# Attention and a routed mixture of experts: the first expert's first 512 rows in two slots, one of them gathered during the attention

## The chip, the cores and the metric

The kernel runs on one core of a Trainium2 chip. The metric is the device time of one execution in microseconds (us). Of the kernel before there are three runs and one profiled execution.

The engines are called by the names of the profile: PE is TensorE, whose weight loads have a row of their own (PEld), ACT is ScalarE, DVE is VectorE, POOL is GpSimd and SP is SyncE. SP computes nothing here: it issues transfers. POOL computes a little and issues the indirect transfers, gathers and scatters, whose rows are named by an index each.

## The reference

The input `x` has B = 4 elements (batches) of T = 1024 rows of C = 256 numbers. What is computed, cut to what matters:

```python
# 1. attention, 16 heads of 16, causal, keys and queries from down- and up-projections, half of each head rotated
x = layernorm(x + attention(x))
# 2. a mixture of 8 experts, two for each row
scores = (x @ router_w.T + router_b) / temperature     # (b, t, 8)
for _ in range(3):                                      # Sinkhorn, over experts and then over rows
    log_alpha = log_alpha - logsumexp(log_alpha, axis=-1)
    log_alpha = log_alpha - logsumexp(log_alpha, axis=-2)
gates = exp(log_alpha) / (sum + 1e-08)
topk_gates, topk_idx = top_k(gates, 2)                  # renormalised
out_e = (relu(x @ wg[e]) * (x @ wp[e])) @ wo[e]         # 256 -> 512 -> 256
x = layernorm(x + sum over the two picks of gate * out_e)
```

The Sinkhorn normalisation runs over the 1024 rows of an element, so the experts of an element's rows are known only when the attention of the whole element is done. It also spreads the rows evenly: an expert gets about 256 pairs (row, expert) of each element.

## The kernel before, in words

**Order.** All engines' instructions are put in order by a scheduler when the kernel is built, from the order in which the program issues them, their priorities and estimated durations. The program is written as generators ("lanes") that yield a cost after each step; the attention loop hands out budgets to them. A step's place on its engine is fixed from then on: an engine runs in order, and where one instruction waits, all behind it wait.

**Attention.** The main loop (L1152 to L1217) goes over units of four heads, four units per element; in the last element, b = 3, the later half of the queries is done first, then the first half in two units. In each, scores and exponentials (`s`, `sT`, `pT`) and the products with the values (`y`, L440) alternate, and masks are put on by POOL (`pT`, L478). Beside the attention of element b run the end of element b - 1 (`finish`, L585: projection, layer norm, its rows stored to `x1_rows` and `results`, router logits) and its routing (`route`, L711). SP loads queries and keys (`qs`, `ks`, L339).

**Routing.** `route` does three rounds of Sinkhorn steps, each with turns of PE (`sk_tp`, L774), ACT and DVE, then the top two, then positions: each pair (row, expert) gets a place in its expert's region of a list `pairs` in memory. `so_ps` (L840 to L845, PE) counts the pairs ahead of each, `base` (L852, DVE) is the number of places used by the elements so far, `so_i` (L863) the index. `scatter` (L866) writes the pairs of an element there with 16 indirect transfers on POOL (L873), as `S0` to `S3` in the lane `places`. After element 2, `base` is raised to 512 for each expert (`floor`, L853), so that the first 512 places of each region hold pairs of elements 0 to 2 alone, and can be worked on while element 3 is still routed.

**Slots.** The experts' work is cut into slots: eight `first` ones of 512 rows (the first 512 places of the eight regions), eight `second` ones (places 512 to 1023), and 256-row slots for what lies beyond, of which three always run. A slot

- takes its list: one load on SP for all eight first slots (`ents`, L974), one for the second eight, and one for each 256-row slot (`ent`, L967);
- gathers its rows with one indirect transfer per 128 rows (`xg`, L985, POOL; two buffers);
- loads its weights (L1011, SP, three transfers of 512 KB) and splits them into high and low halves (`wh` on ACT L191, `wl` on DVE L192), six of each per expert;
- transposes its rows on PE (`xgT_ps`, L1030) and splits them (`xh`, `xl`);
- for each of four quarters of the 512 hidden numbers multiplies into `gp` and `lp` (three fp32 matmuls for each product, L198 to L200), then relu and product (L1047 ACT, L1048 DVE), and the halves `hh` and `hl`;
- multiplies by `wo` into `eo`, scales by the gate (L1065, ACT), and adds the result to `results` with an indirect transfer (L1066, POOL). These adds wait for those of the slot before.

The rows, lists and halves of a slot are prepared between the quarters of the slot before it (`begin`, L1235). In slots of 512 rows `gp` and `lp` have a PSUM bank each, in slots of 256 rows they share one.

**The first slot and the end of the attention.** `begin_early` (L1145) issues the list's load, the weights' loads and the gather of the first slot. The main loop calls it (L1208) when the routing of element 2 is done and all its scatters are out, and if that doesn't come to pass, it is called after the loop. The transposes of the first slot follow (`rows(first[0], ...)`), then the pools of the attention are closed, the split weights go where its buffers were, and the slots begin. What is left of element 3, `finish`, `route` and the table of slots (`lay_out`), is issued here.

**The second eight slots.** The scatters of element 3 (`S3`) are handed out in the slots 0_5 and 0_6 by the table `PLACES`, and what is left at the end of slot 0_6. The load of the second list waits for the last of them, and the gathers of the second slots wait for this list. The order of the second slots is 1_7, 1_6, ... 1_0; the first has the weights of 0_7.

After the last slot the results are read back, added and normalised (L1268 and following).

Of the kernel before, what the change touches and what calls it, by code (L numbers as in the profile page):

```python
# [12 lines left out]
I32 = mybir.dt.int32  # L13
# [20 lines left out]
P = 128  # L34
# [7 lines left out]
def kernel(  # L42
# [16 lines left out]
    nc = tc.nc  # L59
    B, T, C = x_in.shape  # L60
# [3 lines left out]
    E, _, FF = wg_in.shape  # L64
# [11 lines left out]
    scale = 1.0 / math.sqrt(DH)  # L76

    BT = B * T


    ER = 512
    SR = 256
    REGION = BT + SR
    NOVER = (2 * BT - 4 * ER + 2 * (SR - 1)) // SR
    NLIST = (E - 1) * REGION + 2 * ER + NOVER * SR
    NLIST += -NLIST % P

    const = ctx.enter_context(tc.tile_pool(name="const", bufs=1))
# [59 lines left out]
    for half in range(NQC):  # L148
# [13 lines left out]
        out=mask, in_=mask, pattern=[[-1, P]], compare_op=ALU.is_ge, fill=MASKED, base=0, channel_multiplier=1,  # L162
# [5 lines left out]
        out=reach, in_=reach, pattern=[[1, P]], compare_op=ALU.is_ge, fill=MASKED, base=0, channel_multiplier=-1,  # L168
# [34 lines left out]
    for n in range(3):  # L203
        acc = any_tile(f"weffT{n}")
        for i in range(H // 2):
            at = i % 4 * 2 * DH
# [287 lines left out]
    pairs = dram.tile([NLIST, 4], I32, name="pairs")  # L494
    results = dram.tile([BT + ER, C], F32, name="results")
    x1_rows = dram.tile([BT, C], F32, name="x1_rows")

    rank = const.tile([P, E], F32, name="rank")
    base = const.tile([P, E], F32, name="base")
    floor = const.tile([P, E], F32, name="floor")  # L500
    for e in range(E):
# [10 lines left out]
        out=before, in_=before, pattern=[[1, P]], compare_op=ALU.is_gt,  # L512
# [7 lines left out]
    def prepare():  # L520
# [10 lines left out]
        nc.vector.tensor_single_scalar(no_pair[:, :, 0], no_pair[:, :, 3], ER - 1, ALU.bitwise_and)  # L531
        nc.vector.tensor_single_scalar(no_pair[:, :, 1], no_pair[:, :, 0], BT, ALU.bitwise_or)
        nc.vector.memset(no_pair[:, :, 2:4], 0)
        nc.gpsimd.dma_start(out=pairs.rearrange("(p n) w -> p n w", p=P), in_=no_pair)
        nc.gpsimd.dma_start(
            out=results[BT:].rearrange("(n p) c -> p n c", p=P),
            in_=none.unsqueeze(1).to_broadcast([P, ER // P, C]),
# [38 lines left out]
    def apart(what, kind, ins, others):  # L576

        seen = no_deps.setdefault(what, {})
        for o in others:
            for i in seen.get(o, ()):  # L580
                tc.declare_no_dep(ins.ins, i, reason="they touch rows of their own")
        seen.setdefault(kind, []).append(ins.ins)
# [127 lines left out]
    def route(b):  # L710
# [9 lines left out]
        for it in range(SINKHORN_ITERS):  # L720
            m = tiny("sk_m")
# [7 lines left out]
            s = tiny("sk_s")  # L729
# [33 lines left out]
                out=ws, in0=tp[:E, P : 2 * P], in1=wt, scale=1.0, scalar=0.0, op0=ALU.mult, op1=ALU.add,  # L763
# [16 lines left out]
        s = tiny("tk_s")  # L780
# [12 lines left out]
        for k in range(2):  # L793
            m = tiny(f"tk_m{k}")
# [55 lines left out]
        )  # L850
        yield 0.0
        nc.vector.tensor_tensor(base, base, ps[:, NE : NE + E], ALU.add)  # L852
        if b == B - 2:  # L853
            nc.vector.tensor_tensor(base, base, floor, ALU.max)
        at = sinkp.tile([P, 2, NB], F32, tag="so_a", name=f"so_a{b}")
# [11 lines left out]
    def scatter(b, ent, ati):  # L867

        for n in range(NB):
            for k in range(2):  # L870
                while not hole[0]:
                    yield WAIT
                ins = nc.gpsimd.indirect_dma_start(  # L873
                    out=pairs[:, :],
                    out_offset=bass.IndirectOffsetOnAxis(ap=ati[:, k, n : n + 1], axis=0),
                    in_=ent[:, n, k, :], in_offset=None,
                )
                in_turn(ins)
                after(ins, latest[0])
                apart("pairs", "last" if b == B - 1 else "write", ins, ("last", "write", "early"))  # L880
                yield 1.0 if b == B - 1 else SCAT3 if ending[0] else SCAT


    def tab(name, shape):
# [66 lines left out]
    class Slot:  # L951


        def __init__(self, which, s):
            self.which, self.s, self.name = which, s, f"{which}_{s}"
            self.rows = SR if which == 2 else ER
            self.blocks = self.rows // P
            self.raw, self.hl = [None] * 3, [None] * 3
            self.like = None

    lists = {}

    def pairs_of(k):
        if k.which == 2:
            row = value(1, k.s, NLIST - SR)
            k.ent = const.tile([P, k.blocks, 4], I32, name=f"ent_{k.name}")
            nc.sync.dma_start(  # L967
                out=k.ent, in_=pairs[bass.ds(row, SR)].rearrange("(p j) w -> p j w", j=k.blocks)
            )
            return  # L970
        if k.which not in lists:
            ent = lists[k.which] = const.tile([P, E, k.blocks, 4], I32, name=f"ents{k.which}")
            regions = pairs[: E * REGION].rearrange("(e r) w -> e r w", r=REGION)
            ins = nc.sync.dma_start(  # L974
                out=ent.rearrange("p e j w -> p e (j w)"),
                in_=regions[:, k.which * ER : (k.which + 1) * ER].rearrange("e (p j) w -> p e (j w)", p=P),
            )
            if not k.which:
                apart("pairs", "early", ins, ("last",))
        k.ent = lists[k.which][:, k.s]  # L980
# [102 lines left out]
    def drain(gen):  # L1083
        for _ in gen:
            pass
# [41 lines left out]
    early = project(1, 0, bg_tile)  # L1127
# [6 lines left out]
    lane, side, places = Lane(), Lane(), Lane()  # L1134
# [2 lines left out]
    lane.add("prepare", prepare())  # L1137
    budget = {0: (8.0, 8.0, 8.0, 11.3), 1: (9.5, 9.5, 6.0, 11.3), 2: (9.5, 9.5, 6.0, 0.0)}
    budget[B - 1] = (12.0, 4.0, 0.0, 0.0, 8.0, 8.0)
    first = [Slot(0, e) for e in range(E)]  # L1140
    second = [Slot(1, e) for e in reversed(range(E))]
    second[0].like = first[-1]
    further = [Slot(2, n) for n in range(NOVER)]
    early = None
# [7 lines left out]
    routed = [0]  # L1152
    ahead = sum(len(gs) * sum(HG * BPQ * (qc + 1) for qc in qcs) for _, gs, qcs in units)
    for i, unit in enumerate(units):
        b, gs, qcs = unit
        g = gs[0]
        last = b == B - 1
        nth = i - [u[0] for u in units].index(b)
        ends = last and qcs == (0,)
        if nth == 0 and b > 0:  # L1160
            if b == 1:
                lane.until("P2h0")
            elif b == 2:
                lane.until("P3h0")
            lane.add(f"F{b - 1}", finish(b - 1))
            if b + 1 < B:
                lane.add(f"P{b + 1}", project(b + 1, 1, bg_tile))
            if last:
                lane.until(f"P{b}")
                pctx.close()  # L1170
                late_pool[0] = pctx.enter_context(tc.tile_pool(name="late", bufs=1, reuse_waits="tile"))
        if nth == (2 if last else 1) and b > 0:
            lane.until(f"F{b - 1}")
        if ends and g == 0:
            lane.add("F", finish(b, range(1, NQC)))
        if g == 3 and b + 2 < B:
            lane.add(f"P{b + 2}h0", project(b + 2, 0, bg_tile))
        steps = len(gs) * sum(HG * BPQ * (qc + 1) for qc in qcs)
        give = budget[b][nth]
        for n, over in enumerate(attend(unit)):  # L1180
            attended_to += not over
            if i + 2 < len(units):
                if units[i + 2][0] != units[i + 1][0]:
                    if n == 30:
                        lane.until(f"P{b + 1}")
                        load_stack(units[i + 2])
                elif n == 4:
                    load_stack(units[i + 2])

            lead = min(LEAD, HG * BPQ + 2 * attended_to, SLIM + 0.65 * max(0, ahead - 64 - attended_to))  # L1190
            while maxed < attended_to + lead:
                with tc.high_priority(offset=PR[0]):
                    step = next(maxima, None)
                if step is None:
                    break
                maxed += step
            with tc.high_priority(offset=PR[1]):
                lane.give(give / steps)
            if routed[0] < b and not any(m == f"F{b - 1}" for m, _ in lane.todo):
                routed[0] = b  # L1200
                side.add("R", route(b - 1))
            at = n - HG * BPQ * (len(qcs) - 1)
            hole[0] = ends or qcs[-1] > 0 and HOLE[0] <= at < HOLE[1]
            ending[0] = ends
            with tc.high_priority(offset=PR[2] if last else 0):
                side.give(SIDE3 if last else SIDE)
                places.give(1.0)
            if last and routed[0] == b and not side.todo and not places.todo and early is None:  # L1208
                early = pctx.enter_context(early_pool())
                begin_early()  # L1210
        if nth == NG - 1:
            attended[b] = True
# [4 lines left out]
    if early is None:  # L1217
        early = pctx.enter_context(early_pool())
# [35 lines left out]
    def run(keys, given=()):  # L1254
        drain(begin(keys, 0, given))
        for n, key in enumerate(keys):
            slot(key, begin(keys, n + 1, given))
            if key is first[E - 2]:
                places.until(f"S{B - 1}")

    run(first + second + further[:SURE], (0,))
# [134 lines left out]
```

## Time and profile before

| | us |
|---|---|
| median of three runs | 1074.82 |
| the three runs | 1073.68, 1074.82, 1082.69 |
| the profiled execution, its own time | 1075.18 |
| its span in the profile | 1073.4 |
| PE busy in the span | 976.7 (91%) |
| DVE busy | 734.0 (68%) |
| ACT busy | 626.3 (58%) |
| POOL busy | 476.0 (44%) |
| last y matmul of the attention, first gp matmul | 696.31, 697.96 |
| first and last scatter of element 3 (start) | 808.56, 842.44 |
| first transpose of the second list's rows | 852.07 |

The profiled execution took 1.8 us more than its span, which runs from the first to the last instruction that was recorded. Times in the views are microseconds from the start of the span. In a timeline a row has the start, the duration of the group, the engine, line, operation, output and inputs with their shapes, and how many instructions were taken together; in brackets stands how long the engine was idle before it, and what it waited for. "PEclk" is the clock that was granted to PE, in tenths of full speed or as a share. A matmul's start-to-start distance tells what it costs; its own duration is longer, since matmuls are pipelined.

### The profile page before, as it was taken

How to read it: one execution, taken by the hardware profiler on the slowest of the kernel's cores; microseconds unless marked ns; L12 is line 12 of the kernel's file. 1: busy time of each engine (PE TensorE's matmuls, PEld its weight loads, DVE VectorE, ACT ScalarE, POOL GpSimd, SP SyncE). 2: the span in 40 equal slices, each digit the busy share in tenths (PEclk: the TensorE clock that was granted, in tenths of full speed). 3: DMA queues.
4: the chain of work that ended last, by engine and by line, in shares of the span. 5: the costliest groups of instructions: out<-in, count | busy, mean ns of one | idle time of the engine just before them, and what ended most of it. 6: DMA issues, size and time to landing. Idle time of an engine off the chain costs nothing.

```text
span 1073.4 us, 18121 instructions
## 1 busy us (share of the span) xinstructions
PE 976.7 (91%) x6440; PEld 608.2 (57%) x6440; DVE 734.0 (68%) x1627; ACT 626.3 (58%) x1314; POOL 476.0 (44%) x543
## 2 busy tenths in 40 slices
PE   5688999999999999999999998999999699999960
PEld 3554443455544445543344344488888588888860
DVE  4777877888888888798657884085767245555636
ACT  3445666765666656676656675565656245555633
POOL 6174261121352622453233215526557675664535
PEclk9899999999989999999999999899999799999995
DMA  6563331220330412323332220356653464755637
GB/s 252 167 214 96 111 107 35 80 95 26 129 93 33 124 48 73 114 55 109 81 104 84 52 80 2 87 181 159 149 140 92 97 143 110 185 115 125 142 58 313
DMA packets 71363, 119.67 MB, mean 111 GB/s; under 512 B 16416, under 2 KB 43040, under 8 KB 70880
## 3 DMA queue, kind: packets, MB, share of 16 engines
q1 hardware_dynamic: 48544, 81.76, 24.0%
q0 software_dynamic: 20672, 36.41, 15.5%
q8 instruction: 53, 0.87, 0.3%
q10 hardware_dynamic: 2048, 0.27, 0.2%
q14 instruction: 46, 0.38, 0.1%
HBM read 82.52 MB, written 35.60 MB: 110 GB/s over the span
## 4 chain that ended last, share of the span: by engine, by line
PE 76%; DVE 6%; DMA 6%; ACT 5%; issue 3%; SPq 3%; POOL 1%; ACTq 0%; POOLq 0%; DVEq 0%
PE y L440 14%; PE s L354 11%; PE sT L460 11%; PE gp L200 3%; PE gp L199 3%; PE eo L198 3%; PE gp L198 3%; PE eo L199 3%; PE eo L200 3%; PE po L640 3%; SPq L339 2%; ACT pT L471 2%; PE lp L200 2%; PE lp L199 2%; PE lp L198 2%
## 5 line engine op out<-in xcount | busy, mean ns | idle before, releaser
L471 ACT ACTIVATE pT<-sT 128x512 f32<-128x512 f32 (+1 forms) x608 | 327.8, 576 | 175.5 <-PE sT L460 125.4
L375 DVE TENSOR_REDUCE mx<-s 128x1 f32<-128x384 f32 (+3 forms) x352 | 216.3, 633 | 34.9 <-PE s L371 33.5
L460 PE MATMUL sT<-qs,ks 98*128 98x512 bf16 (+3 forms) x768 | 216.4, 331 | 11.3 <-ACT pT L471 8.5
L354 PE MATMUL s<-ks,qs 96*128 96x512 bf16 (+3 forms) x768 | 212.2, 331 | 15.5 <-DMA ks<-parts 8.3
L384 DVE TENSOR_REDUCE mx<-s 128x1 f32<-128x512 f32 x256 | 171.2, 682 | 43.6 <-PE s L354 41.0
L478 POOL TENSOR_SCALAR_AFFINE_SELECT pT<-pT 128x512 f32<-128x512 f32 x112 | 70.8, 638 | 253.3 <-ACT pT L471 245.7
L440 PE MATMUL y<-pT,va 128*32 128x512 f32 (+3 forms) x1536 | 172.8, 505 | 2.4 <-POOL pT L478 1.5
L1066 POOL DMA_INDIRECT results<-eo,ents x64 | 104.6, 1635 | 80.2 <-ACT eo L1065 60.6
L354 PEld LDWEIGHTS <-qs 96*128 96x128 bf16 x768 | 71.0, 99 | 120.6 <-issue 90.6
L460 PEld LDWEIGHTS <-ks 98*128 98x128 bf16 x768 | 70.2, 100 | 90.1 <-issue 58.0
L873 POOL DMA_INDIRECT pairs<-ent,so_i x64 | 67.9, 1061 | 67.5 <-ACT pT L471 49.2
L1048 DVE TENSOR_TENSOR relu<-relu,lp 128x512 f32<-128x512 f32 x64 | 43.8, 685 | 63.2 <-PE lp L200 33.1
L371 PE MATMUL s<-mask,ident_b 128*128 128x128 bf16 (+2 forms) x352 | 86.6, 247 | 0.0
L192 DVE TENSOR_TENSOR wl<-w,wh 128x512 fp32r<-128x512 f32 x108 | 69.7, 684 | 19.6 <-ACT wh L191 17.1
L198 PE MATMUL eo<-wh,hh 128*128 128x256 f32 x280 | 81.2, 291 | 0.9 <-ACT eo L1065 0.6
L199 PE MATMUL eo<-wl,hh 128*128 128x256 f32 x280 | 79.4, 285 | 0.0
L985 POOL DMA_INDIRECT xg<-x_rows,ents x64 | 64.5, 1008 | 33.5 <-issue 17.0
L1047 ACT ACTIVATE relu<-gp 128x512 f32<-128x512 f32 (+1 forms) x76 | 42.8, 563 | 62.4 <-PE gp L200 38.4
L200 PE MATMUL eo<-wh,hl 128*128 128x256 f32 x280 | 77.8, 284 | 0.0
L440 PEld LDWEIGHTS y<-pT,va 128*32 128x32 f32 x1536 | 32.2, 108 | 63.5 <-issue 44.5
L191 ACT CAST wh<-w 128x512 fp32r<-128x512 f32 x108 | 60.4, 618 | 11.0 <-PE gp L199 7.3
L192 DVE TENSOR_TENSOR hl<-relu,hh 128x512 fp32r<-128x512 f32 (+1 forms) x76 | 48.6, 647 | 26.3 <-ACT hh L191 21.3
(222 smaller groups left out, 1870.9 us busy)
## 6 DMA issues: line engine op xcount, KB each, us to landing
ks<-parts SPq DMA_DIRECT2D x90, 128.0 KB
w<-in_wg_dram SPq DMA_DIRECT2D x18, 512.0 KB
w<-in_wp_dram SPq DMA_DIRECT2D x18, 512.0 KB
w<-in_wo_dram SPq DMA_DIRECT2D x18, 512.0 KB
qs<-parts SPq DMA_DIRECT2D x66, 128.0 KB
parts<-lv POOLq DMA_DIRECT2D x12, 384.0 KB
parts<-lv POOLq DMA_DIRECT2D x24, 192.0 KB
xh<-in_x_t_dram SPq DMA_DIRECT2D x8, 512.0 KB
```

Source lines behind the costliest of these rows:

```text
L192: (sub or nc.vector).tensor_tensor(lo, src, hi.bitcast(F32), ALU.subtract)
L198: nc.tensor.matmul(ps, lhsT=sh, rhs=mh, start=(i == 0), stop=False)
L199: nc.tensor.matmul(ps, lhsT=sh, rhs=ml, start=False, stop=False)
L200: nc.tensor.matmul(ps, lhsT=sl, rhs=mh, start=False, stop=(i == n - 1))
L354: nc.tensor.matmul(ps, lhsT=q(h, half)[:NROW, t * P : (t + 1) * P], rhs=k(h, kc)[:NROW, :w], start=first, stop=last,)
L371: nc.tensor.matmul(each[:, :, w - P :], lhsT=ident_b, rhs=mask.unsqueeze(1).to_broadcast([P, m, P]), start=False, stop=True,)
L375: nc.vector.tensor_reduce(mx_of[:, half, h0 : h0 + m, t], each, AX.X, ALU.max)
L384: nc.vector.tensor_reduce(mx_of[:, kc, h, t : t + 1], ps, AX.X, ALU.max)
L440: nc.tensor.matmul(acc[g, qc][SLOT * h : SLOT * (h + 1), lo:], lhsT=va[b % 2][:, kb, at : at + SLOT], rhs=pT[:, h, lo:], start=(kb == 0), ...
L460: nc.tensor.matmul(st[:, h % m * w : (h % m + 1) * w], lhsT=k(h, kb // BPQ)[: NROW + 2, kb % BPQ * P : (kb % BPQ + 1) * P], rhs=q(h, qc)[: ...
L471: latest[0] = nc.scalar.activation(pT[:, h + 1 - m : h + 1, lo:], st[:, : m * w].rearrange("p (h t) -> p h t", t=w), AF.Exp, scale=scale,)
L1066: ins = nc.gpsimd.indirect_dma_start(out=results[:, :], out_offset=bass.IndirectOffsetOnAxis(ap=k.ent[:, j, 1:2], axis=0), in_=eo, in_offs ...
```

## The change

The first expert's first 512 places are worked on in two slots of 256 rows, 0_0 and 0_256. After element 1, `base` of expert 0 is raised to at least SR = 256, so that the first 256 places of its region hold pairs of elements 0 and 1 alone. The load of this slot's list is issued at the end of the scatters of element 1, and `begin_early` is called as soon as the loop, in its last element and past the first of its units, finds these scatters gone. Slot 0_256 has a list load and a gather of its own and uses the split weights of slot 0_0. The list `ents` of all first slots is loaded as before, now for 0_1 and the following. Scatters of element 2 and 3 and the list loads have kinds that say which of them touch different places, so that they don't wait for each other. There are nine first slots instead of eight, and the rest of the scatters of element 3 is issued after the last but one of them, which is 0_6 as before.

```diff
@@ route
         nc.vector.tensor_tensor(base, base, ps[:, NE : NE + E], ALU.add)
+        if b == B - 3:
+            nc.vector.tensor_scalar_max(base[:, :1], base[:, :1], float(SR))
         if b == B - 2:
             nc.vector.tensor_tensor(base, base, floor, ALU.max)
@@ scatter
-                apart("pairs", "last" if b == B - 1 else "write", ins, ("last", "write", "early"))
+                kind = "last" if b == B - 1 else "last but one" if b == B - 2 else "write"
+                apart(
+                    "pairs", kind, ins,
+                    ("last", "last but one", "write", "first") + (("early",) if b == B - 1 else ()),
+                )
                 yield 1.0 if b == B - 1 else SCAT3 if ending[0] else SCAT
+        if b == B - 3:
+            pairs_of(first[0])
@@ Slot
-        def __init__(self, which, s):
-            self.which, self.s, self.name = which, s, f"{which}_{s}"
-            self.rows = SR if which == 2 else ER
+        def __init__(self, which, s, at=None):
+            self.which, self.s, self.name, self.at = which, s, f"{which}_{s}" if at is None else f"{which}_{s}_{at}", at
+            self.rows, self.ent = ER if which < 2 and at is None else SR, None
@@ pairs_of
+        if k.ent is not None:
+            return
...
+        if k.at is not None:
+            row = k.s * REGION + k.at
+            k.ent = const.tile([P, k.blocks, 4], I32, name=f"ent_{k.name}")
+            ins = nc.sync.dma_start(
+                out=k.ent, in_=pairs[row : row + k.rows].rearrange("(p j) w -> p j w", j=k.blocks)
+            )
+            if not k.which:
+                apart("pairs", "early" if k.at else "first", ins, ("last",) if k.at else ("last", "last but one"))
+            return
@@ the slots
-    first = [Slot(0, e) for e in range(E)]
+    first = [Slot(0, 0, 0), Slot(0, 0, SR)] + [Slot(0, e) for e in range(1, E)]
+    first[1].like = first[0]
     second = [Slot(1, e) for e in reversed(range(E))]
@@ the main loop
-            if last and routed[0] == b and not side.todo and not places.todo and early is None:
+            if last and nth and not any(m == f"S{B - 3}" for m, _ in places.todo) and early is None:
                 early = pctx.enter_context(early_pool())
                 begin_early()
@@ run
-            if key is first[E - 2]:
+            if key is first[-2]:
                 places.until(f"S{B - 1}")
```

## The prediction

> **What bounds the kernel now.** I read first the slices of the page, to see where TensorE (PE) is not the bound; then, for each of the two holes that the change can reach, the engine's timeline and the chain of waits.
>
> ```profile
> PE   5688999999999999999999998999999699999960
> PEclk9899999999989999999999999899999799999995
> ```
>
> A slice is 26.8 us, the first is slice 0. PE is at 90% or more from slice 4 to 37, but for slice 24 (644 to 671, in the last stretch of the attention) and slice 31 (832 to 859), which is a 6 at clock 7. That hole is the place where the first eight slots give way to the second eight. The chain of waits there:
>
> ```profile
> 829.84 0.37 SPq L1011
> 830.21 14.85 issue
> 845.05 3.26 DMA ents<-pairs
> 848.44 0.73 issue
> 849.17 1.00 POOL xg L985
> ...
> 853.00 2.65 DMA xg<-x_rows,ents
> 855.78 0.47 PE xgT_ps L1030
> ```
>
> SP stands 14.85 us at the load of the second list until the last scatter of the last element has landed; then come the list (3.26 us) and the gathers. POOL's timeline shows what those scatters (L873) wait for:
>
> ```profile
> 806.67 1.58 POOL L1066 DMA_INDIRECT results<-eo,ents  x1 [4.22 <-ACT eo L1065]
> 808.56 1.47 POOL L873 DMA_INDIRECT pairs<-ent,so_i  x1 [0.30 <-DVE upto L905]
> 810.33 2.60 POOL L873 DMA_INDIRECT pairs<-ent,so_i  x1 [0.30 <-issue]
> 813.23 2.37 POOL L873 DMA_INDIRECT pairs<-ent,so_i  x1 [0.30 <-issue]
> 815.91 0.96 POOL L873 DMA_INDIRECT pairs<-ent,so_i  x1 [0.30 <-issue]
> ...
> 842.44 0.98 POOL L873 DMA_INDIRECT pairs<-ent,so_i  x1 [0.30 <-issue]
> ```
>
> POOL goes without a break from 806.67 to 843.42: 16 scatters and five result scatters between them. So the hole's end is set by when POOL begins them and how fast it goes. PE pays:
>
> ```profile
> 852.07 0.45 PE L1030 MATMUL xgT_ps<-ident,xg 128*128 128x128 f32 x1 [7.10 <-DMA xg<-x_rows,ents]
> ...
> 855.78 0.47 PE L1030 MATMUL xgT_ps<-ident,xg 128*128 128x128 f32 x1 [0.76 <-DMA xg<-x_rows,ents]
> ...
> 856.27 0.41 PE L199 MATMUL eo<-wl,hh 128*128 128x256 f32 x1
> ```
>
> Its last matmul before started at 844.57, so nearly 11 us go until the fourth transpose, and then the matmuls of eo are 0.21 us apart instead of 0.12 until about 860.5 (granted clock 0.50 in 850 to 860): 2.0 us more. The other hole is the end of attention, where transposes of the gathered rows stand among the last y matmuls:
>
> ```profile
> 695.27 0.63 PE L440 MATMUL y<-pT,va 128*32 128x256 f32 x6 [0.82 <-ACT pT L471]
> ...
> 696.66 0.55 PE L1030 MATMUL xgT_ps<-ident,xg 128*128 128x128 f32 x3
> ...
> 697.96 0.49 PE L198 MATMUL gp<-xh,wh 128*128 128x512 f32 x1
> ```
>
> **The change part by part.** I set the compiled orders of both kernels side by side, engine by engine.
>
> Early gather. The list of slot 0_0 (SP) and its two gathers (POOL) now stand behind the scatters of element 1, whose last is issued at 611.60. The last scatter of element 3 lands 2.6 us after its issue (842.44 to 845.05), so SP gets past the new load at about 614.2. Behind it on SP stand the six ks loads that wait for PE until 614.61 anyway: cover 0.4 us; without it, attention waits a few us for ks at most. On POOL the gathers come at about 617.5 to 620, ahead of a mask (affine select) that starts at 618.78 after 4.12 us of idle time; it may come 1 us late, and the next one is due only at 622.09. Taken: 0; bounds 0 to 1.5 us, as PE is busy 10 of 10 there.
>
> End of attention. The eight transposes of xg_0 and three of xg_1 leave PE's order between y and the first gp: four pairs of 0.38 to 0.44 and one group of 0.55 us, 2.2 us in all. Four of them go to 678 to 682, where PE has half the clock and ScalarE (ACT) sets the pace. First gp then at 695.9 instead of 697.96: a gain of 2.1. Lower bound 0: ACT's wh casts start at 697.28, right behind its last yT, and could keep the end where it is; upper bound 3.5: the 0.82 of waiting and some of ACT's 3.88 us wait on the transposes (before 694.62) go too.
>
> Slots 0_0 and 0_256 in place of one. 96 matmuls at 256 columns for 48 at 512: 96 x 0.118 less 48 x 0.233 (starts of eo and of gp in the timeline) = +0.1 us. ACT: four more relu and hh at 376 and 396 ns for four at 597 and 620, two more xh: +1.0 us; VectorE (DVE) the same way (418 for 685): +0.7 to 1.2. DVE is 5.00 of 5 us busy in 700 to 705 and 4.98 in 710 to 715, PE 4.94 and 5.00: both bind. Taken 0.5; bounds 0 to 1.2. The new maximum on base is one DVE instruction of 128x1 behind a row of 0.16 us; nothing waits there: 0.
>
> Route of element 3. On PE its positions (so_ps) move ahead of gp_5_0, from behind lp_5_2. By the sum of PE's rows from the first gp, 88.5 instead of 100.2 us; before, that took 6.3 us more than the sum (697.96 + 100.2 = 798.2, but 804.47), so after: 695.9 + 88.5 + 5.6 + 0.5 = 790.5, 14 earlier.
>
> Scatters of element 3. They can't use all of that: POOL has xg_7's gathers and eo_4_0 ahead of them (800.83 before), so 800.83 - 2.1 + 1.57 + 0.3 = 800.6 for the first, 8.0 earlier. Up to the last one's start the order has 15 scatters and four result scatters (4_1, 4_2, 4_3, 5_0; five before). Pitch: the first five take 1.98 each (808.56 to 818.44), the others 1.40; a result scatter 1.9. Sum 5 x 1.98 + 10 x 1.40 + 4 x 1.9 = 31.5: the last is issued at 832.1 (842.44), its data there at 834.7, first gather at 838.8 (849.17), first transpose possible at 841.7, the fourth at 845.4 (855.78).
>
> PE at the second list. It arrives after 137.6 us of rows (139.6 before; 12 matmuls of gp_7_3 and lp_7_3 are moved behind the transposes): 695.9 + 137.6 + 7.4 + 0.5 = 841.4, where 7.4 is the 844.97 - 697.96 - 139.6 of before. So it meets the first block on time and waits three times 0.75 us, to 845.4. From there to the next point that is the same in both orders (transposes of slot 1_6, 872.78 before) are 17.7 us of rows (15.0 before, plus the 2.0 of half clock = 17.0 seen). So 863.1 at full clock, 9.7 earlier; 865.1 with the same loss of clock, 7.7 earlier. Before, stretches with a pause and matmuls between (695 to 698) kept clock 1.00, but 11 us of almost nothing did not; I take the middle, 8.7.
>
> The Trainium skill, "TensorE: Matmul & The Clock Gate", Part 1: The HAM clock gate, says that a window of about 3.4 us without work halves the clock and a busy one restores it; 0.50 in 850 to 860 and 0.97 in 860 to 870 agree. By it a wait of 4 us with four transposes in it need not halve the clock, and the gain would be 9.7, not 8.7.
>
> From 872.78 to the end PE is the bound and the orders are the same, so the gain stays: 1075.18 - 8.7 = 1066.5 against the profiled execution, which is 0.36 above the median of the three runs: **1066.1 us**.
>
> **The rivals.** (a) Scatters at full rate. At the end of attention the same kind of scatters go at 1.26 us (648 to 654). Then the last is issued at 800.6 + 15 x 1.26 + 4 x 1.9 = 827.1, gathers from 833.8, first transpose possible 836.7, before PE arrives at 841.4: no wait, 1_6 at 841.4 + 17.7 + 0.5 = 859.6, gain 13.2: 1061.6. For it: the rows of 0.96 us after 815.91. Against: scatters between result scatters took 1.40.
>
> (b) Scatters slow throughout. The two of 2.60 and 2.37 us fall in 808 to 816, with DVE 7.93 of 8 us busy; element 3's scatters now begin 8 us earlier, next to other DVE work. All at 1.98: last issued 800.6 + 15 x 1.98 + 7.6 = 837.9, fourth transpose 851.2, 1_6 at 870.9 with the loss of clock, gain 1.9: 1072.9. The Trainium skill, "SBUF — State Buffer", SBUF: two separate sides, says that GpSimd can't write its descriptors while DVE holds the port that they share; the two long rows agree, the 0.96 us ones beside an idle DVE too. The same end has the case that the scatters begin no earlier than before, since POOL or ACT holds them: 1073 to 1075.6.
>
> (c) Slower. PE runs in order. Before, so_m was there at 800.28 and PE took it at 804.47, 4.2 us of reserve; now PE comes to it 14 us earlier, while the logits that start the chain come 2.1 + 6.7 = 8.8 earlier and DVE has 3.5 us less of rows ahead of it: reserve about 2.5. If the Sinkhorn steps (each with a turn of PE, DVE and ACT) run later than that, PE stands in slot 4, with all matmuls behind. Up to some 3 us hide in the wait at the second list; from 13 us of lag on the kernel is slower than before, from 24 us by 1%. For 15 us: 1077.
>
> **How the numbers follow.** About 1% (10.75 us) is what a measurement of this kernel tells from no change. Chances: forecast (gain 4 to 10.7) 0.50; (a) 0.26; (b), with the scatters that begin no earlier, 0.16; (c) 0.08, half of it past 1%. Faster by over 1% (below 1064.1) is (a) and a little of the forecast's upper end: 0.30; slower by over 1%: 0.05; within: 0.65. Range: from (a) with the 1.1 us more at the end of attention, 1060.5, to the upper end of (b), 1075.0.
>
> **What would show it.** Right: two gathers at L985 between 615 and 621; no x_rows transposes in 687 to 696 and the first gp at 695 to 697; so_ps near 790 with no idle time of PE before it; the first scatter of element 3 at 800 to 801, the last near 832; PE's wait before the second list's transposes under 5 us instead of 11, and clock above 0.8 there. Wrong: idle time of PE "<-DVE so_m" or "<-DMA ks"; scatters of 2 us throughout; a first gp at 698; DVE as what ends PE's idle time in 700 to 720.

## The result, and the profile after

| | before | changed |
|---|---|---|
| median of the runs beside each other, us | 1076.79 (4 runs) | 1065.97 (4 runs) |
| lowest and highest run, us | 1073.68, 1082.69 | 1061.88, 1070.52 |
| the profiled execution and its span, us | 1075.18, 1073.4 | 1070.52, 1068.7 |
| first gp matmul | 697.96 | 696.04 |
| first and last scatter of element 3 (start) | 808.56, 842.44 | 801.59, 829.67 |
| transposes of slot 1_6 begin | 872.62 | 867.26 |

The ratio is 0.9899, 95% interval 0.9871 to 0.9928: about 1% faster. The profiled execution of the changed kernel is the longest of its four runs and gained only 4.7 us, so this profile shows less gain than the median. The lines of the changed kernel stand lower in the file, by 1 in the attention and in the matmuls of the slots (L199 to L201), by 3 at the scatters of pairs (L876), by 20 in the slots (gathers L1005, transposes L1050, result scatters L1086); in e2 it is two less there, in e5 and e9 to e12 one less.

The slices of the page, changed kernel: the 6 at slice 31 (now 828 to 855) is an 8 with the clock at 9, and slice 25 (668 to 695) has become an 8 beside slice 24.

```profile
PE   6688999999999999999999998899999899999960
PEclk9889999999999999999999999999999999999985
```

The end of the attention on PE's timeline, changed kernel:

```profile
691.91 0.55 PE L615 MATMUL yt_ps<-ident,yT 128*128 128x128 f32 x3
694.38 0.43 PE L441 MATMUL y<-pT,va 128*32 128x128 f32 x8 [1.93 <-ACT pT L472]
694.74 0.44 PE L1050 MATMUL xgT_ps<-ident,xg 128*128 128x128 f32 x2
...
696.04 0.38 PE L199 MATMUL gp<-xh,wh 128*128 128x256 f32 x1
```

The four transposes of slot 0_0 are gone from here (two each at 681.18 and 682.64); the two that are left at 694.74 are of slot 0_256, so the sign of none in 687 to 696 isn't met to the letter. PE stands 1.93 us for ACT before the last y products.

POOL's timeline, changed kernel: the early gather, then the first and the last scatter of element 3 and the first gather of the second list.

```profile
618.63 1.04 POOL L1005 DMA_INDIRECT xg<-x_rows,ent  x1 [1.80 <-DMA ent<-pairs]
619.98 0.96 POOL L1005 DMA_INDIRECT xg<-x_rows,ent  x1 [0.31 <-issue]
620.95 0.64 POOL L479 TENSOR_SCALAR_AFFINE_SELECT pT<-pT 128x512 f32<-128x512 f32 x1
```

```profile
801.59 1.27 POOL L876 DMA_INDIRECT pairs<-ent,so_i  x1 [0.30 <-issue]
...
829.67 0.95 POOL L876 DMA_INDIRECT pairs<-ent,so_i  x1 [0.30 <-issue]
...
836.66 1.01 POOL L1005 DMA_INDIRECT xg<-x_rows,ents  x1 [1.48 <-PE xgT_ps L1050]
```

PE's timeline, changed kernel: the second half of the transposes of slot 0_7, which still has its rows from the first list, and then the first transposes of the second list's rows.

```profile
834.03 0.80 PE L199 MATMUL gp<-xh,wh 128*128 128x512 f32 x1 [2.67 <-ACT xh L192]
...
835.48 1.06 PE L1050 MATMUL xgT_ps<-ident,xg 128*128 128x128 f32 x4
...
848.68 0.60 PE L1050 MATMUL xgT_ps<-ident,xg 128*128 128x128 f32 x4
```

The group at 835.48 is what the first gather of the second list (836.66) waited for. The second list's own four transposes, at 848.68, run as one group without a wait for their rows. But PE had stood 2.67 us for ACT at 834.03, 0.77 and 1.22 us at 811.63 and 814.19, and 0.52 at 829.28: it came to the list late. Whether that belongs to the change was the first question.

### The profile page after: what moved, and what is told of

Same layout as the page of the kernel before. It is cut to its first block, busy times and chain, and to the rows that moved or that the text cites. A ratio compares the mean times of both kernels' runs of the same rounds, so it can differ in the third digit from the quotient of the medians.

```text
span 1068.7 us, 18250 instructions
## 1 busy us (share of the span) xinstructions
PE 973.5 (91%) x6488; PEld 609.0 (57%) x6488; DVE 736.0 (69%) x1638; ACT 626.9 (59%) x1324; POOL 477.4 (45%) x543
## 4 chain that ended last, share of the span: by engine, by line
PE 77%; DVE 6%; DMA 6%; ACT 4%; SPq 3%; issue 2%; POOL 1%; another core or an unknown queue 0%; ACTq 0%; POOLq 0%; DVEq 0%
PE y L441 13%; PE s L355 11%; PE sT L461 10%; PE gp L201 4%; PE gp L200 3%; PE gp L199 3%; PE eo L201 3%; PE eo L199 3%; PE eo L200 3%; PE po L641 3%; SPq L340 3%; PE lp L201 2%; PE lp L200 2%; PE lp L199 2%; ACT pT L472 2%; PE s L372 2%
## 5 line engine op out<-in xcount | busy, mean ns | idle before, releaser
L441 PE MATMUL y<-pT,va 128*32 128x512 f32 (+3 forms) x1536 | 169.9, 500 | 3.6 <-ACT pT L472 1.9
L355 PEld LDWEIGHTS <-qs 96*128 96x128 bf16 x768 | 71.2, 99 | 123.1 <-issue 93.8
L1086 POOL DMA_INDIRECT results<-eo,ents x60 | 100.4, 1673 | 73.4 <-ACT eo L1085 60.3
L876 POOL DMA_INDIRECT pairs<-ent,so_i x64 | 64.3, 1004 | 68.4 <-ACT pT L472 50.1
L1068 DVE TENSOR_TENSOR relu<-relu,lp 128x512 f32<-128x512 f32 x60 | 41.0, 684 | 66.4 <-PE lp L201 25.2
L199 PE MATMUL eo<-wh,hh 128*128 128x256 f32 x280 | 80.7, 290 | 1.3 <-ACT eo L1085 1.3
L201 PE MATMUL eo<-wh,hl 128*128 128x256 f32 x280 | 77.9, 284 | 0.0
L1005 POOL DMA_INDIRECT xg<-x_rows,ents x60 | 61.9, 1031 | 30.3 <-issue 15.2
L199 PE MATMUL gp<-xh,wh 128*128 128x512 f32 (+1 forms) x200 | 70.9, 360 | 2.8 <-ACT xh L192 2.7
L200 PE MATMUL gp<-xl,wh 128*128 128x512 f32 (+1 forms) x200 | 71.6, 359 | 0.0
L201 PE MATMUL gp<-xh,wl 128*128 128x512 f32 (+1 forms) x200 | 70.6, 355 | 0.3 <-DVE wl L193 0.3
```

Of the source, the lines that this page charges most:

```text
L199: nc.tensor.matmul(ps, lhsT=sh, rhs=mh, start=(i == 0), stop=False)
L200: nc.tensor.matmul(ps, lhsT=sh, rhs=ml, start=False, stop=False)
L201: nc.tensor.matmul(ps, lhsT=sl, rhs=mh, start=False, stop=(i == n - 1))
L355: nc.tensor.matmul(ps, lhsT=q(h, half)[:NROW, t * P : (t + 1) * P], rhs=k(h, kc)[:NROW, :w], start=first, stop=last,)
L441: nc.tensor.matmul(acc[g, qc][SLOT * h : SLOT * (h + 1), lo:], lhsT=va[b % 2][:, kb, at : at + SLOT], rhs=pT[:, h, lo:], start=(kb == 0), ...
L1086: ins = nc.gpsimd.indirect_dma_start(out=results[:, :], out_offset=bass.IndirectOffsetOnAxis(ap=k.ent[:, j, 1:2], axis=0), in_=eo, in_offs ...
```

## The experiments

Each has five rounds, with the kernel before on the same chip. The ratios are to that; e1 to e4 ran together on one chip, e5 to e7, e8 to e10 and e11 to e12 on three others.

**e1: the changed kernel once more.**

> The changed kernel as it is, for a second profile. Theory A (what the profile after shows is built into the order of its instructions): about 10 us faster than before (1062 to 1070); PE again stands about 5 us in the stretch in which slot 0_6 passes to 0_7 (808 to 836 in the first profile), among it 2 to 3 us for ACT's xh, and doesn't wait for the second list. Theory B (those waits were an accident of that run): PE's waits there under 1.5 us, and the time nearer to 1062.

1059.01 us against 1072.70, ratio 0.9862 (0.9835 to 0.9888). PE's timeline:

```profile
688.79 0.44 PE L1050 MATMUL xgT_ps<-ident,xg 128*128 128x128 f32 x2
689.57 0.66 PE L615 MATMUL yt_ps<-ident,yT 128*128 128x128 f32 x4 [0.34 <-ACT yT L446]
690.09 0.38 PE L199 MATMUL gp<-xh,wh 128*128 128x256 f32 x1
```

```profile
835.59 0.90 PE L1050 MATMUL xgT_ps<-ident,xg 128*128 128x128 f32 x3 [1.73 <-DMA xg<-x_rows,ents]
837.02 0.48 PE L1050 MATMUL xgT_ps<-ident,xg 128*128 128x128 f32 x1 [0.54 <-DMA xg<-x_rows,ents]
837.15 0.56 PE L199 MATMUL eo<-wh,hh 128*128 128x256 f32 x1
837.51 0.41 PE L200 MATMUL eo<-wl,hh 128*128 128x256 f32 x1
```

The first gp comes at 690.09, 6 us earlier than in the first profile, with no stand ahead of the last y products; and none of the four stands in the slots is there. So the stands don't follow from the order of the instructions, which is the same. What is there is a wait of 1.73 + 0.54 us for the second list's rows, and after it matmuls 0.21 us apart. The stretches of this profile (the first number after the stretch's length is PE's busy time, the one ahead of the DMA share the granted clock) confirm the half clock:

```profile
830.00:835.00 5.00, 3.85 (x17) 2.78 (x15) 2.16 (x4) 1.75 (x4) 3.81 (x4) 1.00 1.09 357
835.00:840.00 5.00, 3.88 (x17) 3.40 (x18) 1.30 (x2) 1.10 (x2) 3.78 (x5) 0.66 0.49 104
840.00:845.00 5.00, 5.00 (x29) 4.26 (x29) 2.84 (x5) 3.17 (x6) 4.08 (x4) 1.00 0.49 128
```

POOL's timeline in e1, the scatters of element 3 from the first to the last (821.80):

```profile
794.32 1.00 POOL L876 DMA_INDIRECT pairs<-ent,so_i  x1 [0.30 <-DMA xg<-x_rows,ents]
...
821.80 2.59 POOL L876 DMA_INDIRECT pairs<-ent,so_i  x1 [0.30 <-issue]
...
830.28 1.01 POOL L1005 DMA_INDIRECT xg<-x_rows,ents  x1 [2.13 <-PE eo L201]
```

They take 27.5 us, mostly 1.27 apart, with four result scatters between them.

**e2: the two slots, without the early gather.** List, gather and transposes of slot 0_0 come behind the scatters of element 2, as in the kernel before; all else keeps its order.

```diff
-        if b == B - 3:
-            pairs_of(first[0])
...
-            if last and nth and not any(m == f"S{B - 3}" for m, _ in places.todo) and early is None:
+            if last and routed[0] == b and not side.todo and not places.todo and early is None:
```

> The changed kernel with two slots of 256 rows, but list, gather and transposes of slot 0_0 are where those of the first slot were before: behind the scatters of element 2. All else keeps its order on every engine. Theory A (the early gather frees the end of the attention): 2 to 5 us slower than the changed kernel, first gp 2 to 5 us later, and the rest unchanged. Rival (the split alone, by the order of the slots behind it, brings the gain): within 1 us of the changed kernel, about 10 faster than before.

1063.65 us, ratio 0.9895 (0.9867 to 0.9923): 4.6 us over e1. PE's timeline:

```profile
683.93 0.69 PE L1048 MATMUL xgT_ps<-ident,xg 128*128 128x128 f32 x2 [2.03 <-DMA xg<-x_rows,ent]
...
685.83 1.94 PE L441 MATMUL y<-pT,va 128*32 128x512 f32 x8
...
695.70 0.39 PE L199 MATMUL gp<-xh,wh 128*128 128x256 f32 x1
```

PE waits 2.03 us for the gathered rows, and then eight y matmuls take 1.94 us where the same ones take 1.07 us at full clock (687.09 in the first profile). The first gp is 5.6 us later than in e1: 2.0 are the wait, and 3.6 are left for the transposes and the slower clock. The kernel before (its orders, in e3) shows the same wait on this chip:

```profile
687.25 0.69 PE L1030 MATMUL xgT_ps<-ident,xg 128*128 128x128 f32 x2 [2.22 <-DMA xg<-x_rows,ents]
```

The order of the slots and scatters alone, e2 against the kernel before, is worth the other 9.1 us. The traces put it behind the attention: from the start of element 2's last scatter to the first gp both take 20.6 us (675.13 to 695.70 in e2, 677.83 to 698.45 in e3), but from the first gp to the first scatter of element 3 it is 104.1 us in e2 (799.81) and 111.9 in e3 (810.36).

**e3 and e4: half the scatters of element 3,** in the kernel before and in the changed one. The second pick of element 3's rows is left out, so there are 8 scatters and fewer pairs to work on.

```diff
-            for k in range(2):
+            for k in range(1 if b == B - 1 else 2):
```

> The kernel before with 8 instead of 16 scatters of element 3: the second pick of each row of element 3 is left out, so the second list is complete some 14 us earlier; PE, DVE and ACT keep their orders. Theory A (the wait at the second list is worth what it showed, 11 us and 2 us of clock): 10 to 13 us faster than before, 1062 to 1065. Rival (something else, gather buffers or weights, is due right behind): less than 5 us.

> The changed kernel with the same 8 scatters of element 3 left out. Theory A (after the change the second list is no longer waited for, and PE's own waits in slot 0_6 have taken its place): within 1.5 us of the changed kernel. Rival (the list still sets the pace): 3 to 6 us faster than the changed kernel.

e3: 1064.71 us, ratio 0.9918 (0.9893 to 0.9944). e4: 1057.75 us, ratio 0.9858 (0.9831 to 0.9886). In both, the end (from ACT's last eo to the end of the span) is longer than with all scatters, 39.2 and 39.0 us against 35.4 to 36.3, about 3.3; why is not shown, and by the medians alone e3 gains 8.0 us, less than the 10 to 13 of its theory. With the 3.3 added, the hole at the second list cost the kernel before 8.0 + 3.3 = 11.3 us, near the 9.4 of waiting and 2.0 of half clock that its profile shows, and it still costs the changed one 1.3 + 3.3 = 4.6. In the traces, ACT's two eo around the list's transposes are 10.0 us apart in e1 (830.06, 840.03) and 5.7 in e4 (829.73, 835.42), which is 4.3: the 2.3 us of waiting, and 2.0 that are left for the half clock behind it. In e4 PE is busy throughout there, at full clock:

```profile
830.00:840.00 10.00, 10.00 (x59) 8.55 (x58) 5.87 (x9) 5.67 (x11) 8.17 (x7) 1.00 0.54 84
```

So 4.3 to 4.6 us are still to be had at the list. The next runs tried to get them by an earlier last scatter.

**e5, e6, e7, e9: the scatters in long rows,** by the table `PLACES`; only POOL's order (and with it the place of list and weight loads on SP) is another. e5 and e9, the same kernel: 16 in a row.

```diff
-    PLACES = {(f"0_{E - 3}", n): m for n, m in zip(range(NFC), (2, 3, 3, 2))}
-    PLACES |= {(f"0_{E - 2}", n): m for n, m in zip(range(NFC), (2, 2, 2, 0))}
+    PLACES = {(f"0_{E - 5}", 0): 16}
```

e6 keeps the two lines with `E - 4` and `E - 3`, which gives rows of 14 and 2; e7 is the kernel before with the 16 in a row.

> The changed kernel with all 16 scatters of element 3 in a row, ahead of the result scatters eo_4_1 and following; only POOL's order changes, the other engines keep theirs. Theory A (what the changed kernel still loses at the second list, 4.3 to 4.6 us by the comparison with half of the scatters, is the four result scatters that stand between them): last scatter 7 to 8 us earlier, no wait of PE at the second list, 4 to 5 us faster than the changed kernel. Rival (the result scatters, held up by 20 us, run out of their six buffers and stop ACT and PE): a new wait of PE before eo in slots 0_4 and 0_5, gain under 1 us or a loss.

> The changed kernel with 14 scatters of element 3 in a row, then two result scatters, then the last two; only POOL's order changes. Theory A: last scatter about 4 us earlier than in the changed kernel, 3 to 4.5 us faster than it. Rival as in the run with all in a row: under 1 us.

> The kernel before with all 16 scatters of element 3 in a row behind eo_4_1; PE, DVE and ACT keep their orders, on SP three weight loads go behind the second list. Theory A (most of what the split brought at the second list is the earlier end of these scatters, which can be had without the split): last scatter 8 to 10 us earlier, 7 to 10 us faster than before. Rival (the scatters beside dense DVE work take 2 us each throughout): last scatter 4 us earlier, 3 to 4 us faster.

> The changed kernel as it is, as the control for the two runs beside it on the same chip. Both theories: 9 to 14 us faster than before.

> The changed kernel with the 16 scatters of element 3 in a row, again, now beside the changed kernel on one chip. Theory B (a long row of scatters on POOL holds up the other engines): 15 to 25 us slower than the control. Rival C (the loss of the first time was that chip's): within 5 us of the control, as the earlier list would have it.

| | us | ratio, 95% interval |
|---|---|---|
| e5, 16 in a row | 1082.54 | 1.0041 (1.0024 to 1.0059) |
| e6, 14 and 2 | 1080.89 | 1.0032 (1.0013 to 1.0051) |
| e7, before with 16 in a row | 1079.25 | 1.0007 (0.9982 to 1.0031) |
| e8, the changed kernel (control) | 1065.49 | 0.9899 (0.9876 to 0.9921) |
| e9, 16 in a row again, with e8 | 1079.91 | 1.0027 (1.0006 to 1.0048) |

The row costs 14.4 us against its control, more than the whole gain, and in e7 none of the 7 to 10 us comes that the earlier scatters should have brought. In e9 the last scatter and the list did come early (827.86 and 830.02 in e8). POOL and SP in e9:

```profile
800.68 1.26 POOL L876 DMA_INDIRECT pairs<-ent,so_i  x1 [0.30 <-issue]
...
820.98 0.96 POOL L876 DMA_INDIRECT pairs<-ent,so_i  x1 [0.30 <-issue]
```

```profile
823.41 0.37 SPq L993 DMA_DIRECT2D ents<-pairs  x1
```

But the engines stood. ACT's timeline and the stretches of e9 (busy us of PE, weight loads, DVE, ACT and POOL, then the clock):

```profile
817.16 0.62 ACT L192 CAST hh<-relu 128x512 fp32r<-128x512 f32 x1
831.01 0.60 ACT L1066 ACTIVATE relu<-gp 128x512 f32<-128x512 f32 x1 [13.23 <-remote]
```

```profile
815.00:820.00 5.00, 3.51 (x12) 2.57 (x11) 2.07 (x4) 1.10 (x2) 3.78 (x5) 0.52 0.83 224
820.00:825.00 5.00, 4.07 (x17) 3.03 (x15) 0.00 (x0) 0.00 (x0) 4.09 (x4) 0.80 0.07 6
825.00:830.00 5.00, 0.00 (x0) 0.00 (x0) 0.00 (x0) 0.00 (x0) 4.09 (x4) 0.89 0.87 103
```

In 825 to 830 nothing but POOL is busy, and PE's next wait is 6.83 us, on ACT's relu. What ACT itself waited for 13.23 us, the trace doesn't name ("remote"). The stand goes on 9 us after the end of the row (821.94). The rival of e5, that the result scatters held back run out of their six buffers, is not seen in e9: only three wait behind the row (they start at 822.25, 824.15 and 826.03), and ACT's next eo comes after the stand, at 832.95.

**e10 and e11: short rows.** e10 has rows of 6, 5 and 5, e11 of 5, 4, 4 and 3, with one result scatter between two.

```diff
+    PLACES = {('0_4', 4): 6, ('0_4', 5): 5, ('0_4', 6): 5}
...
+    PLACES = {('0_4', 4): 5, ('0_4', 5): 4, ('0_4', 6): 4, ('0_4', 7): 3}
```

> The changed kernel with element 3's scatters in rows of 6, 5 and 5, each followed by one result scatter, so that two result scatters stand ahead of the last scatter instead of four; only POOL's order changes. Theory A with B (rows of up to 6 do no harm, an earlier list helps): last scatter 3.8 us earlier, 2 to 4 us faster than the control. Rival D (any result scatter that comes later costs as much as the list gains): within 1 us of the control or slower.

> The changed kernel with the 16 scatters of element 3 on POOL as rows of 5, 4, 4 and 3 with one result scatter (4_1, 4_2, 4_3) between two rows; the orders of PE, DVE, ACT and SP are the same, and only POOL's differs. The last scatter then stands behind three result scatters instead of four and should start about 1.9 us earlier than in the changed kernel. Theory A, that only rows of more than five hold the other engines up: PE's wait at the second list (2.3 us) goes, the ratio to the kernel before is 0.001 to 0.002 below the changed kernel's 0.986 to 0.990, and PE has no idle time over 1 us between 800 and 830. Theory B, that any packing of the scatters makes the slots beside them later, as the rows of 6 and 5 did (3.0 us over the control): ratio 0.990 to 0.995, with PE waiting 1 to 3 us more for ACT in 805 to 830, which eats what the earlier list gives.

e10: 1068.48 us, ratio 0.9954 (0.9923 to 0.9985), 3.0 us over its control e8. e11: 1065.51 us, ratio 0.9904 (0.9872 to 0.9937), no better than the changed kernel. In e11 the last scatter started at 826.96, 2.7 us before the first profile's, with nearly the same first gp (695.59), and ACT and PE stood again:

```profile
818.44 0.62 ACT L192 CAST hh<-relu 128x512 fp32r<-128x512 f32 x1
829.43 1.09 ACT L1066 ACTIVATE relu<-gp 128x512 f32<-128x512 f32 x2 [10.37 <-remote]
```

e11's six runs lie between 1061.27 and 1078.92, and this profile is of one of 1076.32, so a stand of this size can hardly be in all of them. Theory A of e11 falls; no arrangement that was tried beats the changed kernel.

**e12: eight in a row, half the scatters.** e4 with `PLACES = {(f"0_{E - 5}", 0): 8}`.

> The changed kernel without the second pick of element 3 (8 scatters, and the work that follows from them is left out), and all eight in one row on POOL behind eo_4_0, where e4 has them as 5 and 3 with two result scatters between. PE, DVE and ACT have the same orders as in e4. Theory A, that the cost grows with the length of a row: 16 in a row cost 14 to 18 us, so 8 in a row cost 3 to 8 us beside e4 (ratio 0.9858): 0.989 to 0.993, with PE idle for 3 us or more in 805 to 825. Theory B, that the engines stand only when a row outlasts what they have at hand, about 15 us of a row of 20: no cost, ratio 0.984 to 0.987, no idle time of PE over 1.5 us there.

1070.90 us, ratio 0.9967 (0.9943 to 0.9991), above what both theories had. But the pair is not clean: the first gp comes at 696.22, against 689.79 in e4, and e11 on e12's chip has 695.59. In the slots alone e12 loses 4.7 us to e4 (ACT's eo run 7.7 us behind in the first slots and 12.4 from slot 0_5 on), inside A's 3 to 8. PE stands 1.27 and 1.07 us at 813.52 and 815.55, less than A asked for and within B's 1.5. And without any such row the first profile of the changed kernel loses 5.5 us to e1 in the slots (171.2 and 165.7 us from the first gp to the transposes of slot 1_6). So e12 decides neither theory; its control on the same chip, e4, was not run there.

## Why the prediction came out

The time, 1066.1 against a median of 1065.97, and the range hold. The terms were not all right, and errors of both signs cancelled.

**Early gather, cost 0 (0 to 1.5): right.** The gathers start at 618.63 and 619.98, the mask after them at 620.95; PE's wait there is 0.32 us in e1 and under 0.3 in the first profile.

**End of attention, 2.1 (0 to 3.5): mis-sized, and hit by luck.** The first gp comes 1.9 us earlier in the first pair. But the changed kernel's profile was already 1.9 us late at the first scatter of element 2 (649.73, 647.80). From there to the first gp it is 50.2 us before and 46.3 after, a gain of 3.9; on e1's chip it is 45.9 (e3) and 45.8 (e2) against 40.4 (e1), a gain of 5.5, and 4.6 in the medians of e1 and e2. My sum had the transposes and not the wait for gathered rows that ends last ahead of them. In the profile of before the first transposes start 4.35 us after the first gather (687.43, 683.08), without a wait; in e3 they wait and start 2.87 us after it (687.25, 684.38). So the reserve was 1.5 us. What gave it was PE's half clock, which the prediction had seen at 678 to 682 and taken as given: it was 0.50 from 676.2 to 686.5, which cost PE about 5.1 us. In e2 and e3 the clock is 1.00 there; PE comes too soon, waits 2.03 and 2.22 us, and its clock is halved from the wait on. In e7, the kernel before up to there, the half clock is over at 680.8, and PE waits too:

```profile
688.18 0.44 PE L1029 MATMUL xgT_ps<-ident,xg 128*128 128x128 f32 x2 [1.53 <-DMA xg<-x_rows,ents]
```

That cover was there to be named. It also means that the first pair doesn't show what the early gather is worth: the changed profile has only 3.4 us of half clock in that stretch (659.6 to 663.0) where before had 10.2, and whether that belongs to the change is not shown. The control for it is e2.

**Two slots, 0.5, and the route: right.** From the first gp to so_ps I had 94.6 us; it is 95.1 in the first profile and 93.8 in e1. PE doesn't stand at so_ps: rival (c) is not seen. (ACT's part of the two slots was put at 1.0 us; its rows, 8 x 0.772 less 4 x 1.217, give 1.3 without the xh.)

**Scatters, 31.5 us from first to last: too long.** 28.1 and 27.5 (e1). The 1.98 us of the first five, taken over from before, didn't come back: most stand 1.27 apart, one takes 2.59 us. That is rival (a)'s rate; but its conclusion, no wait at the list, doesn't hold in e1. There the fourth transpose comes 15.2 us after the start of the last scatter (13.3 before), 1.6 of the difference in that scatter itself, and PE comes to the list 143.8 us after the first gp, where I had 145.5. What (b) read is not borne out either: the scatters of 0.96 us don't stand beside an idle DVE, which in the profile of before was busy 1.80 of 5 us in 815 to 820 and 4.21 in 825 to 830.

**PE at the second list: wait right, clock wrong.** Three gaps of 0.75 us were forecast, 2.27 us came (e1). I took half of the loss of clock, 1.0; it was all of it, about 2.0 (0.50 from 836.4 to 839.8). The Trainium skill, "TensorE: Matmul & The Clock Gate", Part 1: The HAM clock gate, by which about 3.4 us without work halve the clock, doesn't lead to that: here an idle time of 1.73 us was followed by 0.50. The measurement decides, though not every wait of that size does it: 1.97 us at 657.01 in the profile of before left the clock at 1.00.

**What the sum lacked:** the stands in the slots beside the scatters, 0.77 + 1.22 + 0.52 + 2.67 = 5.2 us in the first profile, none in e1, with half clock from 833.7 to 837.1 behind the last, about 1.5 us more. With them PE comes to the list 152.6 us after the first gp (848.68) instead of 145.5. They took the place of the wait at the list there, and are most of why the profiled execution gained 4.7 us only. That they are in one execution of the changed kernel and not in another is shown; why is not.

So the mechanism was the forecast's: scatters earlier by the route moved ahead (9.1 us, e2), and the attention's end freed of the gather (4.6 us), the second with a wait that the sum didn't have. The time itself came out so well by luck: the end of the attention gave more than its term, and the stands took it back. (The range's lower end used 1.1 us more at the end of attention; by the term's own bound it is 1.4.) On e1's chip the two come to 13.7 us; in the first pair and with e8 to 10.8 and 10.3.

## What to carry to other kernels

A wait that a profile doesn't show may be hidden by a slow stretch of the same engine just ahead of it, here PE at half clock: compare its reserve (1.5 us) with what that stretch cost (5.1 us), and take the wait in as a bound. After moving a chain forward, look at what stands between its new end and its user (here a list load and four gathers), and count the clock's loss behind each wait of about 2 us as a bound. Before taking the difference of two single profiles for a term, look whether they differ as much ahead of the change. Don't pack indirect transfers into a long row to finish them sooner without a control on the same chip.

## What the runs showed of the hardware

**Stands on some chips and not on one.** On e1 to e4's chip none of the four profiles has PE's stand of about 2 us beside element 2's scatters or that before the attention's end. All other profiles, the kernel before's too, have the first, and those of the changed kernel and its variants the second as well (1.2 to 2.1 us). e8:

```profile
655.51 0.22 PE L468 MATMUL sT<-reach,ident_b 128*128 128x128 bf16 x1
657.66 0.38 PE L461 MATMUL sT<-qs,ks 98*128 98x256 bf16 x2 [1.94 <-ACT pT L472]
```

Ahead of this stand, ACT's pT in e8 starts at 657.12, 2.7 us after the recorded end (654.41) of the matmul that it waits for; in e1 the same pT starts at 655.45, at the end of its matmul (655.41). Some of this can be lost records; the stand itself is in the times of PE's next work. Why it is there is not shown.

**Half clock in spells.** In these traces PE's clock is 0.50 for 3.4 us or a whole multiple of it: 3.4 in e1 (836.4 to 839.8), 6.8 in e2 (683.4 to 690.2), 10.2 and 13.7 in the profile of before (676.2 to 686.5, 846.9 to 860.5). A wait of about 2 us was followed by such a spell in e1 (1.73) and e8 (1.94), but not in the profile of before (1.97 at 657.01) or in e10 (1.96 at 657.64). In the spell of 676.2 to 686.5 PE was busy all the time; why it lasted so long is not shown.

**Long rows of indirect scatters.** 16 in a row, 21 us on POOL, cost 14.4 us (e9 against e8), with PE, ACT and DVE standing, though most of the scatters took their usual 0.96 us. Part of it is the half clock behind the stands (0.50 from 815.2 to 822.0 and from 828.9 to 835.7). PE's own loads of instructions are not the cause: between two of them PE executed 252 instructions in e9, over a gap of 40 us, and 252 and 254 in e1 in the 22.7 and 19.9 us around the same place. So the gap follows from the stand. And no load of instructions of any engine starts in e9 between 811.9 and 841.0, so none ended ACT's stand at 831.01. The cause stays open, and also whether such a row would cost as much on e1's chip, where none was run, and whether any other work of POOL would do the same, which was not tried.
